# Sending the rows of two attentions' factors through DRAM instead of through TensorE, in a planned graph-and-slice transformer layer

## The chip, the core and the metric

The kernel runs on one core of a Trainium2 chip. The metric is device time in microseconds (us) from the start to the end of one execution; of several runs the median is taken. The profile is of one more execution.

## What is computed

The input x has 32 batch items of 512 nodes with 256 features, in fp32; adj is a 512 x 512 mask shared by all. One layer of a graph network and one of a slice transformer follow each other, each with a residual connection:

```python
def _gat(inp, adj_mask, W, a):
    h = inp @ W
    f1, f2 = h @ a[:F, 0], h @ a[F:, 0]
    e = leaky_relu(f1[:, :, None] + f2[:, None, :], 0.2)
    if adj_mask is not None:
        e = where(adj_mask[None] > 0, e, NEG_INF)
    return elu(softmax(e, axis=2) @ h)

def gnn(x):                       # 256 -> 512 -> 256 features
    out = residual = relu(x @ mlp1_w + mlp1_b)
    out = elu(_gat(relu(out), None, W_fc, a_fc)) + residual
    out = residual = relu(out @ mlp2_w + mlp2_b)
    out = elu(_gat(relu(out), adj, W_hand, a_hand)) + residual
    return relu(out)

def ffn(x):                       # 8 heads of 64, 64 slices
    w = softmax((x_mid @ W_slice + b_slice) / temp)     # 512 nodes x 64 slices, per head
    tokens = (fx_mid.T-weighted sums over the nodes) / (sums of w + 1e-5)
    out_slice = attention(tokens @ W_q, tokens @ W_k, tokens @ W_v)
    return (w @ out_slice, heads joined) @ W_out + b_out

x = x + gnn(layernorm(x), adj)
x = x + ffn(layernorm(x))
```

What matters for this change: both attentions add a number of the row's node (f1) and a number of the column's node (f2). A number that lies one to a node, so one to a partition, is at some point needed along a row of 512, the same in all 128 partitions. That is what is called spreading a factor here.

## The kernel before

**The work of one batch item.** `front(b)` loads x, does the first layernorm, mlp1, the product h with a Strassen scheme (seven products instead of eight), the factors, the attention matrix pT in a separable form and its product with h (pv, Strassen again). `middle(b, o1T)` does mlp2, the product h2, the masked attention e, its transposition p2T and the product pv2. `back(b, x1)` does the second layernorm, the slice weights w, the sums, the tokens, the small attention, and the output. Each part sets `nc.step`, one of 22 names from "load" to "out".

**Layout.** A tile has 128 partitions; the 512 nodes are NT = 4 to a partition: node 4p + t lies in partition p, place t, for x and the output. Transposes of large tiles are made without TensorE in the 30 batches other than the first and the last (`by_dma(what, b)` is true for them): VectorE transposes blocks of 32 x 32 (`flip`) into a stage, and `gather` writes the stage to DRAM by four DMAs and reads it back by one. For e this gives e_stage, scr and p2T. In the first and last batch TensorE transposes instead.

**How the factors are spread.** In the step "factors", f1 of the first attention is column HH of h, one number for each partition and place. VectorE adds f2's maximum to it (tile sc, 128 x 4), TensorE transposes each of the four columns, broadcast to 128, against the identity (tr<-ident,sc), and ScalarE reads the resulting PSUM tile pt, 128 x 512, into acb with two activations, then takes the exponential. In the step "h2" column D+1 of h2 goes the same way (tr<-ident,h) into a PSUM tile f2b; VectorE reads it directly for the four instructions that make e, each of which adds f2b to the mask mbias and keeps the row's maximum (e<-tr,mbias); only in the first and the last batch ScalarE first copies it to SBUF.

**What sets the order.** All operations are first recorded (`Recorder.take`; so the profile shows line 343 for nearly all of them), then `_schedule` puts them in one order with costs of its own: at each point it takes, of those that can start, the one with the lowest key, and no item may be more than three batches ahead of the oldest. A key is a due time: batch number times PERIOD, plus a value from the table TURNS by step and place in the step, plus shifts for the first and last three batches from HEAD and TAIL. SETUP holds the keys of the one-time preparations. Each engine then runs its instructions in that order and waits where an input or a buffer is not ready. So the table sets which work of four neighbouring batches stands beside which on every engine. In `emit`, within 120 us of the planned start or end, matmuls on the identity are put in where TensorE is planned to stand idle (`_fill`; line 351 in the profile).

**Queues.** Before the change all DMAs of the batches are issued by SP (SyncE); ScalarE issues two small ones at the very start.

Of the kernel before, what the change touches and what calls it, by code (L numbers as in the profile page):

```python
# [7 lines left out]
F32 = mybir.dt.float32  # L8
I32 = mybir.dt.int32
BF16 = mybir.dt.bfloat16  # L10
AF = mybir.ActivationFunctionType
OP = mybir.AluOpType
# [2 lines left out]
ENGINES = ("tensor", "vector", "scalar", "gpsimd", "sync")  # L15

TURNS = {
    "load": (-104.13,),
    "norm1": (5.81, -12.2, -0.38, 40.46, 5.49, 6.82, -28.3, -97.35, 73.26, 2141.3, -17.24, 7.8,
        -3.21, -61.78, -29.05, -31.03, -34.36, -3.93, -211.23, -208.37, -208.62, -207.57,  # L20
        -202.44),
    "mlp1": (44.88, -14.78, 475.5, -0.81, 29.84, 144.85, 30.48, 28.34, 46.7, 63.76, 30.7,
        163.15),
    "h": (217.43, 239.71, 301.88, 219.38, 228.31, 232.52, 223.78, 123.55, -183.63, -198.06,
        235.55, 281.78, 134.23, 84.93, 296.28, 284.15, 228.15, 213.81, 208.35, 40.76, -192.43,
        -208.97, 324.43, 90.08, 232.1, 162.36, 264.44, 305, 269.96, 302.11, 159.39, 131.88,
        217.06, 97.44, 286.09, 265.51, 197.21, 172.48, 330.83, 139.13, 316.66, 332.6, 199.8,
        210.03, 184.56, 233.17, 252.5, 357.26, 288.33, 243.5, 272.56, 242.46, 243.89, 262.61,
        301.12, 303.21),
    "factors": (1172.98, 68.61, 957.87, 880.81, 833.88, -94.89, 162.9, 564.16, 443.05, 632.16,  # L30
        99.22, 41.55, 117.2, -36.09, 151.35, 166.12, 162.03),
    "p": (-217.52, 222.09, -214.68, 156.3, -232.9, 226.84, -201.59, 222.19),
    "pv": (181.62, 173.02, 113.17, 168.75, 130.31, 121.86, 154.04, 91.05, 128.61, 93.43, 156.55,
        170.07, 249.5, 203.18, 183.65, 209.43, 161.93, 146.07, 129.44, 175.77, 84.33, 98.64,
        193.99, 67.43, 82.92, 77.34, 188.5, 225.33, 179.85, 196.17, 141.96, 66.83, 209.82,
        122.72, 185.96, 166.17, 256.1, 208.95, 191.25, 109.15, 168.68, 33.05, 111.29, 31.79,
        223.06, 225.68, 0.25, 146.41, 143.11, 131.52, 150.56, 135.14, 171.77, 185.87, 148.08,
        129.9, 112.28, 230.93, 210.68, 202.98, 108.67, 123.15, 135.98, 121.57, 427.87, 287.12,
        306.19, 126.95, 47.96, 44.6, 23.6, 354.94, 212.32, 233.37, 145.94, -25.73, 89.65, 87.01,
        301.3, 340.74),  # L40
    "o1": (175.72, 146.36, 318.31, 75.22, 202.48, -123.71, -11.06, -130.7, -287.11),
    "mlp2": (163.2, 216.89, 255.93, 271.92, 60.63, 285.36, 184.81, 130.74, 28.96, 65.99),
    "h2": (154.01, 126.18, 171.55, 124.34, 108.59, 78.41, 169.3, 89.79, 186.32, 157.35, 180.91,
        192.19, 105.96, 124.57, 26.13, 58.76),
    "e": (226.55, 172.24, 227.68, 199.08, 187.7, 234.17, 190.31, 206.45, 237.64, 232.92, 168.72,
        256.08, 408.52, 421.68, 391.27, 262.45, 442.54, 455.27, 273.82, 234.38, 519.53, 170.71,
        164.48, 31.36),
    "p2": (-14.68, 22.01, 55.59, 61.1, 56.92, -11.8, 67.6, 558.07, 85.28, 48.17, 40.53, 30.86,
        19.78, -12.55),
    "pv2": (231.3, 86.58, 94.48, 97.84, -101.11, 186.76, 109.51, 61.52, 85.01, -131.77, -150.14,  # L50
        205.52, 259.66, 267.31, 237.42, -131.44, -160, -120.69, -132.24, 154.68, 148.6, 111.83,
        139, -129.21, 152.77, 106.35, 144.25, 119.14, -162.13, -156.66, 273.74, 322.31, 325.93,
        361.68, -139.88, -151.25, -142.85, -161.55),
    "norm2": (3024.02, 107.62, 108.82, 88.2, 97.55, 53.73, 74.18, 49.61, 117.29, 3167.28,
        180.18, 68.34, 64.85, 86, 21.41, 8.51, 60.74, 13.84, 28.42, 83.96, 129.51, 212.73,
        234.97, 261.11, 2822.4, 116.47),
    "w": (305.34, 272.53, 290.14, 845.93, 798.64, 795.47, 283.65, 884.75, 926.27, 320.18, 751.4,
        375.01, 408.12, 405.42, 336.46, 305.77, 323.75, 367.7, 1201.11, 1138.46, 1563.38,
        745.63, 1124.55, 865.97, 1179.02, 980.75, 363.54, 428.69, 395.78, 437.6, 334.39, 367.5,
        367.07, 981.88, 934.2, 840, 174.53, 1035.96, 203, 1037.78, 1034.98, 480.9, 411.92,  # L60
        442.36, 358.87, 346.56, 246.11, 386.64, 1234.45, 758.39, 808.64, 610.85, 681.86, 882.99,
        492.47, 722.21, 414.99, 446.77, 335.28, 249.32),
    "sums": (219.1, 219.58, 227.77, 239.7, 383.95, 249.92, 251.57, 239.42, 242.03, 1077.37,
        1977.83, 234.3, 1454.25, 735.43, 2640.86, 592.26, 423.25, 660.64, -9.73),
    "s1T": (108.57, 368.64, 346.43, 140.99, 183.21, 126.3),
    "tokens": (328.88, 276.03, 298.43, 280.34, 354.01, 226.15, 295.4, 216.36, 344.5, 310.56,
        213.27, 259.2, 166.72, 280.67, 245.65, 277.29, 211.49, 312.02, 299.07, 271.19, 138.52,
        257, 235.11, 203.31, 251.8, 264.98, 212.57),
    "att": (205559.95, 208057.13, 394.33, 51833.74, 297.35, 190333.7, 260689.92, 418216.35),
    "vo": (374.47, 235.14, 638.61, 320.05, 321.87, 373.17, 345.11, 230.64, 163.72, 211.34,  # L70
        232.93, 232.76, 169.48, 276.17, 419.48, 556.46),
    "gg": (-50.95, -63.34, -63.34, -51.08, -78.74, -66.07, -40.3, -20.46, 150.92, 121.98),
    "out": (158.85, 78.08, -2.92, 6.88, -44.11, -73.16, -25.26, -4.67, 103.63, 87.34, -10.37,
        24.58, -12.49, 48.01, 59.4, 101.43, 136.08, 81.21, 268.69),
}
PERIOD, SPARE = 80.54, 0.01

HEAD = (
    (-61, -359, 0, 40, 0, 69, -1262, 189, -43, 457, -8, -24, 143, 947, 108, 718, -48, 6, 1, -39,
     119, -20),  # L80
    (168, 1, 0, 0, 0, 4, 174, 0, 144, -26, 75, 433, 58, 166, 0, 117, 154, 0, -183, -48, -372,
     1721),
    (172, 728, 1325, 0, -59, -269, -21, 34, -18, -363, 2035, 398, 404, -24, 1613, -199, 25,
     -134, 0, -3, -46, -85),
)
TAIL = (
    (36, 0, -352, 1, 67, 0, -772, 105, -24, 0, -312, 50, -6, -235, 1896, 375, 54, 83, -211, 13,
     -147, -271),
    (18, -170, -262, -383, 0, 42, 11, -11, -950, 795, -14, -10, -1671, -108, -157, 653, 6, 18,
     0, 210, 2, 652),  # L90
    (-4, -40, 0, -69, 10, -43, -630, -53, 276, -593, -1, -10, -589, 151, 299, 42, 316, 15, 89,
     4, -160, 43),
)


SETUP = (791.3598735632129, 2808.359873563213, 4385.359873563213, 9205.359873563213, 6407.359873563213, 3020.359873563213, 4840.359873563213, 5931.359873563213)

FLIPPED = ("xn", "u", "e", "o2", "w", "xn2")

P = 128  # L100
ALPHA = 0.2
MASKED = -(2.0 ** 55)
# [288 lines left out]
def adj_ffn_kernel(  # L391
# [26 lines left out]
    B, N, D = x.shape  # L418
    HID = mlp1_w.shape[1]
    HH = HID // 2  # L420
    NT = N // P
# [15 lines left out]
    def ts(i, n=P):  # L437
        return slice(i * n, (i + 1) * n)

    def new(name, shape, bufs=1, tag=None, dtype=F32):  # L440
        return sbuf.tile(list(shape), dtype, name=name, tag=tag or name, bufs=bufs)
# [4 lines left out]
    def tr_tile(shape):  # L446
        return psum.tile(shape, F32, tag="bank", name="tr", bufs=8)
# [11 lines left out]
    def by_dma(what, b):  # L459

        return what in FLIPPED and b not in EDGES
# [22 lines left out]
    def row(name, shape=(P, 512), tag=None):  # L484
        return new(name, shape, bufs=2, tag=tag)

    def small(name, shape):
        return new(name, shape, bufs=3)
# [249 lines left out]
            u if to is None else m, m, -1.0, u, op0=OP.add, op1=OP.max  # L738
        )

    def front(b):

        nc.step = "load"
# [72 lines left out]
        nc.vector.tensor_copy(f2[:, 2:], h22[:, :, HH])  # L816
        nc.step = "factors"

        fm = small("fm", [P, 1])
        nc.vector.tensor_reduce(fm, f2, axis=AX.X, op=OP.max)  # L820
        pf = sm_tile([P, P])
# [4 lines left out]


        beta = 1.0 - ALPHA
        sc = small("sc", [P, NT])
        nc.vector.tensor_scalar(sc, f1, f2m, None, op0=OP.add)  # L830
        ex = small("ex", [P, 2, NT])
        nc.vector.tensor_scalar(ex[:, 0], f2, f2m, None, op0=OP.subtract)
        nc.vector.tensor_scalar(ex[:, 1], f2, f2m, ALPHA, op0=OP.subtract, op1=OP.mult)
# [3 lines left out]
        nc.vector.memset(h1[:, :, HH], -1.0)  # L837
        nc.vector.memset(h2[:, :, HH], 1.0)

        pt = tr_tile([P, N])  # L840
        for i in range(NT):
            nc.tensor.transpose(pt[:, ts(i)], sc[:, i : i + 1].to_broadcast([P, P]), ident)
        acb = new("acb", [P, 2, N], tag="xnT")
        nc.scalar.activation(acb[:, 0, :], pt, AF.Relu, scale=-beta)
        nc.scalar.activation(acb[:, 1, :], pt, AF.Relu, scale=beta)
        nc.scalar.activation(acb, acb, AF.Exp, scale=-1.0)

        nc.step = "p"
# [61 lines left out]
    def middle(b, o1T):  # L910
# [17 lines left out]
                    pm, o2T[:, k, ts(t)], wh[:, k, :], start=(k == 0), stop=(k == KD - 1)  # L928
                )
            nc.scalar.copy(h[:, t, :], pm)  # L930
        f2b = tr_tile([P, N])
        for j in range(NT):
            nc.tensor.transpose(f2b[:, ts(j)], h[:, j, D + 1 : D + 2].to_broadcast([P, P]), ident)
        if not by_dma("e", b):
            pt, f2b = f2b, new("f2b", [P, N], tag="acb")
            nc.scalar.copy(f2b, pt)
        nc.step = "e"
        pT = new("p2T", [P, NT, N], tag="pT" if b == B - 1 else None)
        if by_dma("e", b):
# [2 lines left out]
        masked = [new("e", [P, N + 2], bufs=4)[:, :N] for i in range(NT)]  # L942
        for i, e in enumerate(masked):
            nc.vector.tensor_tensor_reduce(
                out=e, in0=f2b, in1=mbias[:, i, :], scale=1.0, scalar=3.0 * MASKED,
                op0=OP.add, op1=OP.max, accum_out=top[:, i : i + 1],
            )
        nc.vector.tensor_tensor(top, top, f1, op=OP.add)
# [341 lines left out]
```

## Time and profile before

| | us |
|---|---|
| median of 3 runs | 2467.51 (2467.47 to 2471.15) |
| the profiled execution's own time | 2464.71 |
| its span, first to last instruction | 2462.9 |

| engine | busy, us | share |
|---|---|---|
| PE (TensorE matmuls) | 2442.5 | 99% |
| PEld (weight loads, beside PE) | 1705.3 | 69% |
| DVE (VectorE) | 2096.1 | 85% |
| ACT (ScalarE) | 1428.9 | 58% |
| POOL (GpSimd) | 116.8 | 5% |

A group of instructions is named by what it writes and reads, out<-in, with numbers left out: mm<-wh,o2T is the product h2, mm<-h,p2T is pv2, mm<-h,pT and the like pv, mm<-gg,wT the output, mm<-weff,xn2T w, mm<-w,xn the sums. A matmul in fp32 takes two passes and counts as two instructions; a transpose takes one. Durations of neighbouring matmuls overlap, so times on PE are read from the distance of starts. SPq marks DMA issues of SP. In the chain of waits each piece gives its start, its length and what the engine did.

### The profile page before, as it was taken

What the parts mean: (1) busy time and instruction counts of PE and PEld (TensorE: products, weight loads), DVE (VectorE), ACT (ScalarE), POOL (GpSimd) and SP (SyncE); (2) the same over time, 40 slices, a digit from 0 to 9 for tenths busy, and PEclk for the clock granted to TensorE, in tenths of its full rate; (3) what the DMA queues carried; (4) which work ended last, traced back from release to release, by engine and by line L of the source; (5) the groups of instructions that cost most, each with busy time, mean ns of one, the idle gap of its engine ahead of it and who ended that gap; (6) DMA issues with size and microseconds to landing.
All of it is one profiled execution on the core that took longest, in us unless ns stands there. A gap on an engine that the chain in (4) does not pass through costs nothing.

```text
span 2462.9 us, 35296 instructions
## 1 busy us (share of the span) xinstructions
PE 2442.5 (99%) x11607; PEld 1705.3 (69%) x11607; DVE 2096.1 (85%) x5636; ACT 1428.9 (58%) x3319; POOL 116.8 (5%) x184
## 2 busy tenths in 40 slices
PE   9999999999999999999999999999999999999999
PEld 7766667666676767676766676766767676767666
DVE  8688798888898888898888888888988888998775
ACT  2665556656556555566565566565565555665564
POOL 4000000000000000000000000000000000000000
PEclk9999999999999999999999999999999999999999
DMA  5133565455565455655555664556654556645531
GB/s 176 35 93 100 154 165 163 126 160 140 157 165 144 133 147 149 163 165 136 149 144 144 165 164 130 156 139 154 168 146 134 147 150 161 163 127 143 139 106 54
DMA packets 450047, 348.11 MB, mean 141 GB/s; under 512 B 109381, under 2 KB 374469, under 8 KB 449864
## 3 DMA queue, kind: packets, MB, share of 16 engines
q1 hardware_dynamic: 449334, 345.85, 51.8%
q8 instruction: 92, 1.51, 0.2%
q14 instruction: 91, 0.75, 0.1%
q10 hardware_dynamic: 530, 0.01, 0.0%
HBM read 186.27 MB, written 159.45 MB: 140 GB/s over the span
## 4 chain that ended last, share of the span: by engine, by line
PE 86%; DVE 3%; DMA 2%; ACT 0%; issue 0%; SPq 0%; DVEq 0%
PE mm L343 83%; PE tr L343 3%; DMA p2T<-scr 1%; DVE e L343 0%; DMA rn<-line 0%; DVE v L343 0%; DMA o1T<-scr 0%; SPq L343 0%; DVE e_stage L343 0%; DVE gg L343 0%; DMA scr<-e_stage 0%; DVE mx L343 0%; DVE pT L343 0%; DVE rs L343 0%; DVE xn_stage L343 0%
## 5 line engine op out<-in xcount | busy, mean ns | idle before, releaser
L343 ACT ACTIVATE w<-mm,mx 128x64 f32<-128x64 f32 x1024 | 231.1, 346 | 41.7 <-DVE mx L343 41.7
L343 PE MATMUL mm<-weff,xn2T 128*128 128x512 f32 x512 | 247.2, 598 | 0.5 <-ACT xn2T L343 0.5
L343 PE MATMUL mm<-w,xn 128*128 128x512 f32 x512 | 235.9, 593 | 3.5 <-DVE w L343 3.5
L343 PE MATMUL mm<-o1T,w 128*128 128x512 f32 x512 | 235.1, 593 | 1.3 <-DVE o1T L343 1.3
L343 PE MATMUL mm<-h,p2T 128*128 128x257 f32 x1024 | 232.5, 380 | 0.9 <-DMA p2T<-scr 0.9
L343 PE MATMUL mm<-gg,wT 128*128 128x256 f32 x1024 | 231.4, 382 | 0.2 <-DVE gg L343 0.2
L343 PE MATMUL mm<-xnT,w 128*128 128x512 f32 x512 | 225.9, 593 | 0.5 <-ACT xnT L343 0.4
L343 PEld LDWEIGHTS mm<-h,p2T 128*128 128x128 f32 x1024 | 193.7, 189 | 42.5 <-issue 14.5
L343 PEld LDWEIGHTS mm<-gg,wT 128*128 128x128 f32 x1024 | 190.0, 190 | 46.4 <-DVE gg L343 22.1
L343 ACT ACTIVATE v<-v,rd 128x512 f32<-128x512 f32 x128 | 90.5, 713 | 172.9 <-DVE rd L343 172.9
L343 PEld LDWEIGHTS mm<-xnT,w 128*128 128x128 f32 x512 | 96.9, 190 | 119.2 <-issue 111.2
L343 ACT ACTIVATE above<-e,top 128x512 f32<-128x512 f32 x128 | 88.4, 720 | 126.1 <-DVE top L343 109.4
L343 PEld LDWEIGHTS mm<-w,xn 128*128 128x128 f32 x512 | 96.1, 190 | 87.9 <-issue 72.3
L343 PEld LDWEIGHTS mm<-o1T,w 128*128 128x128 f32 x512 | 94.6, 190 | 85.9 <-issue 73.4
L343 PEld LDWEIGHTS mm<-weff,xn2T 128*128 128x128 f32 x512 | 93.8, 189 | 70.4 <-issue 56.4
L343 PEld LDWEIGHTS mm<-h,pT 128*128 128x128 f32 x512 | 96.3, 189 | 64.6 <-issue 37.9
L343 ACT ACTIVATE m<-m,neg 128x512 f32<-128x512 f32 x192 | 137.3, 717 | 1.3
L343 PE MATMUL mm<-h,pT 128*128 128x257 f32 x512 | 134.6, 380 | 3.4 <-DVE pT L343 3.4
L343 DVE TENSOR_TENSOR v<-mm,v 128x256 f32<-128x256 f32 (+1 forms) x320 | 127.7, 409 | 3.5 <-PE mm L343 1.7
L343 PE MATMUL mm<-wh,o2T 128*128 128x258 f32 x512 | 127.4, 382 | 0.0
L343 PE MATMUL mm<-h,pmix 128*128 128x256 f32 x512 | 125.8, 378 | 0.0
L343 PE MATMUL mm<-wfc,o0T 128*128 128x257 f32 x512 | 125.0, 385 | 0.0
(191 smaller groups left out, 5002.2 us busy)
## 6 DMA issues: line engine op xcount, KB each, us to landing
scr<-xn_stage SPq DMA_DIRECT2D x240, 128.0 KB, 3.0
scr<-u_stage SPq DMA_DIRECT2D x120, 256.0 KB, 4.4
o1T<-scr SPq DMA_DIRECT2D x30, 1024.0 KB, 7.6
scr<-e_stage SPq DMA_DIRECT2D x120, 256.0 KB, 4.3
p2T<-scr SPq DMA_DIRECT2D x30, 1024.0 KB, 5.4
scr<-w_stage SPq DMA_DIRECT2D x120, 256.0 KB, 4.0
w_raw<-scr SPq DMA_DIRECT2D x30, 1024.0 KB, 7.8
x<-in_x_dram SPq DMA_DIRECT2D x32, 512.0 KB, 4.2
```

Of the source, the lines that this page charges most:

```text
L343: getattr(getattr(self.nc, op.engine), op.method)(*op.args, **op.kwargs)
```

## The change

In the 30 middle batches both factors are spread by two DMAs from ScalarE's queue instead of by four transposes: `spread` writes the 128 x 4 column tile to a line of 512 numbers in DRAM (16 bytes from each partition), and reads that line into each of 128 partitions (2 KB each, tiles f1_row and f2_row, one buffer each). Since the line holds node 4p + t at its place in order, it is read with a step of four elements: `(i t) -> t i`. In the first and the last batch the transposes stay.

For the first attention sc is now f1 alone, copied before f2's maximum is known, and the maximum enters as a bias (fb, two columns) of ScalarE's two activations. For the second a small tile g2 is copied out of h2 first. The four instructions of e read f2_row from SBUF.

All of TURNS, PERIOD, HEAD, TAIL and SETUP is new. The shifts in HEAD and TAIL are nearly all zero, and PERIOD goes from 80.54 to 75.21.

```diff
-PERIOD, SPARE = 80.54, 0.01
+PERIOD, SPARE = 75.21301149425301, 0.01
...
+    def spread(name, col):
+
+        line = dram.tile([P, NT], F32, name="line", tag=name + "_line", bufs=2)
+        nc.scalar.dma_start(line, col)
+        wide = new(name + "_row", [P, N])
+        nc.scalar.dma_start(
+            wide, bass.AP(tensor=line.tensor, offset=line.offset, ap=[[0, P], [1, N]])
+        )
+        return wide.rearrange("p (i t) -> p t i", t=NT)
...
         nc.step = "factors"
 
+        sc = small("sc", [P, NT])
+        nc.vector.tensor_copy(sc, f1)
+        if by_dma("u", b):
+            pt = spread("f1", sc)
         fm = small("fm", [P, 1])
...
-        sc = small("sc", [P, NT])
-        nc.vector.tensor_scalar(sc, f1, f2m, None, op0=OP.add)
+        fb = small("fb", [P, 2])
+        for s, slope in enumerate((-beta, beta)):
+            nc.vector.tensor_scalar(fb[:, s : s + 1], f2m, slope, None, op0=OP.mult)
...
-        pt = tr_tile([P, N])
-        for i in range(NT):
-            nc.tensor.transpose(pt[:, ts(i)], sc[:, i : i + 1].to_broadcast([P, P]), ident)
+        if not by_dma("u", b):
+            pt = tr_tile([P, N])
+            for i in range(NT):
+                nc.tensor.transpose(pt[:, ts(i)], sc[:, i : i + 1].to_broadcast([P, P]), ident)
+            pt = pt.rearrange("p (t i) -> p t i", t=NT)
         acb = new("acb", [P, 2, N], tag="xnT")
-        nc.scalar.activation(acb[:, 0, :], pt, AF.Relu, scale=-beta)
-        nc.scalar.activation(acb[:, 1, :], pt, AF.Relu, scale=beta)
+        for s, slope in enumerate((-beta, beta)):
+            nc.scalar.activation(
+                acb[:, s, :].rearrange("p (t i) -> p t i", t=NT), pt, AF.Relu,
+                bias=fb[:, s : s + 1], scale=slope,
+            )
...
-        f2b = tr_tile([P, N])
-        for j in range(NT):
-            nc.tensor.transpose(f2b[:, ts(j)], h[:, j, D + 1 : D + 2].to_broadcast([P, P]), ident)
-        if not by_dma("e", b):
-            pt, f2b = f2b, new("f2b", [P, N], tag="acb")
+        if by_dma("e", b):
+            f2 = small("g2", [P, NT])
+            nc.vector.tensor_copy(f2, h[:, :, D + 1])
+            f2b = spread("f2", f2)
+        else:
+            pt, f2b = tr_tile([P, N]), row("f2b", tag="u")
+            for j in range(NT):
+                nc.tensor.transpose(
+                    pt[:, ts(j)], h[:, j, D + 1 : D + 2].to_broadcast([P, P]), ident
+                )
             nc.scalar.copy(f2b, pt)
+            f2b = f2b.rearrange("p (t i) -> p t i", t=NT)
...
             nc.vector.tensor_tensor_reduce(
-                out=e, in0=f2b, in1=mbias[:, i, :], scale=1.0, scalar=3.0 * MASKED,
+                out=e.rearrange("p (t i) -> p t i", t=NT), in0=f2b,
+                in1=mbias[:, i, :].rearrange("p (t i) -> p t i", t=NT), scale=1.0, scalar=3.0 * MASKED,
                 op0=OP.add, op1=OP.max, accum_out=top[:, i : i + 1],
             )
```

## The prediction

> **What bounds the kernel now.** First the page's engine line and the table of stretches. PE is busy in all of a middle period, DVE in 65.3 of its 74.6 us, ACT in 44.2.
>
> ```profile
> PE 2442.5 (99%) x11607; PEld 1705.3 (69%) x11607; DVE 2096.1 (85%) x5636; ACT 1428.9 (58%) x3319; POOL 116.8 (5%) x184
> ```
>
> ```profile
> core 0: us, PE busy (x) PEld busy (x) DVE busy (x) ACT busy (x) POOL busy (x), PEclk, DMA share, GB/s
> ...
> 1196.10:1270.70 74.60, 74.60 (x353) 51.83 (x353) 65.29 (x176) 44.18 (x104) 2.91 (x5) 1.00 0.56 150
> ```
>
> Second the chain that ended last: the same piece of matmuls comes back every 74.68 us, one batch, and nearly all of it is PE.
>
> ```profile
> 1121.38 63.52 PE mm L343 x278
> 1196.07 63.52 PE mm L343 x278
> 1270.75 63.52 PE mm L343 x278
> ```
>
> 23 such periods lie between 374.58 and 2092.99; 32 times 74.68 are 2389.8 of the span of 2462.9. So a saved PE pass counts at once, until another loop is as long as the period. The candidate is the second attention: from the last pass of h2 (mm<-wh,o2T) over e, the exchange through DRAM and back to the first mm<-h,p2T. The timelines of PE, DVE and SP give its points:
>
> ```profile
> 1195.02 0.47 PE L343 MATMUL mm<-attT,tokT 64*64 64x64 f32 x16
> ...
> 1226.61 5.37 PE L343 MATMUL mm<-h,p2T 128*128 128x257 f32 x24
> ```
>
> ```profile
> 1196.11 0.69 DVE L343 CUSTOM_DVE_ANT_0 e<-tr,mbias 128x512 f32<-128x512 f32 x1 [0.26 <-PE tr L343]
> ...
> 1212.73 0.69 DVE L343 STREAM_TRANSPOSE e_stage<-e 128x512 f32<-128x512 f32 x1
> ```
>
> ```profile
> 1213.45 3.38 SPq L343 DMA_DIRECT2D scr<-e_stage  x4
> 1220.44 0.38 SPq L343 DMA_DIRECT2D p2T<-scr  x1
> ```
>
> h2 ends at 1195.02, e runs from 1196.11 to 1213.42, and p2T, issued at 1220.44 and landing after 5.4 us (its median), is there at 1225.84, **0.8 us before PE asks for it** at 1226.61. In one period the chain of waits shows this loop running out:
>
> ```profile
> 1364.76 4.92 DMA scr<-e_stage
> 1369.70 6.76 DMA p2T<-scr
> 1376.46 0.14 issue
> 1376.59 8.47 PE mm L343 x35
> ```
>
> 1226.61 plus two periods is 1375.97, so PE began 0.6 us late there.
>
> [...] SP stood 124.6 us in 29 waits for line<-norm, the same construction. [...] The trace of before has no such read on DVE or ACT; on POOL the one read at that step (mbias<-adjt) takes 2.11 us beside 0.83 for mbias<-mbias, in other types.
>
> **The change part by part.** (a) In 30 batches four transposes of sc and four of h2's last column go. Pieces of four transposes take 0.44 us in the chain of waits, so 8 x 0.11 = 0.87 us a batch, 26 us in all, on PE: the floor of the period becomes 73.81.
>
> (b) ACT loses nothing (in the 30 middle batches DVE read f2b from PSUM without a copy) and gains four DMA issues a batch. The two ACT issues at the start of the trace took 0.47 and 0.49 us; line<-norm, with the same pieces of 16 bytes, 1.06 on SP at the median. So 2 to 3 us of ACT's 30 idle ones. Behind the waiting f1_row issue stand xn2's two copies and o2T's relu, which PE needs for h2; behind line<-g2 stand two pT, a few exps and the copy of mean, which PE needs for mm<-wvo,mean. By the order of instructions these have about 0.3 us to spare, so I put 0 to 0.6 us a period, and take 0.2.
>
> (c) The pair of DMAs. norm<-s1T, equally 2 KB, lands after 2.8 us; the broadcast m<-W_fx, equally 128x512 from one row, after 3.3, in the quiet start. f1's loop (h to pT's matmuls) has mlp2, h2, w, wvo, out and half of sums on PE between, 29 us at the steps of (d), and needs about 11 (issue 0.5, the DMAs 6.1, acb 2.2, pT 1.3, signals); those hide it. f2's isn't roomy. Its loop in the new order of instructions: fourth h2 copy behind attT's 0.8; g2 0.3; line issue 0.5; two pT, mean and eight exps on ACT (3.2) end at 4.8, later than the line's landing (1.1 + 2.8 = 3.9); f2_row's landing 3.3 and the signal give 8.3. DVE from the first e to the last flip, at the steps of its timeline: four e 2.4, four max 2.3, five flips 3.1, three statistics 1.0, two mx 1.2, two w 1.2, two x1 1.2, rs and pmix 1.2, small ones 0.5: 14.1, to 22.4 (before, 17.3, with pT and gg between). From the last flip to p2T's landing as before, 1213.42 to 1225.84: 12.4. **Sum 34.8.**
>
> (d) What PE does meanwhile in the new order, counted at the steps of the PE timeline: 32 passes of 512 (w, sums) at 0.43, 13.8; 32 of out, 7.05; 56 of the Strassen product of pv at 0.217, 12.15; wvo 1.04, attT 0.40, tokens 1.08, a transpose 0.11: **35.6**. So p2T would be 0.8 us early, if nothing of (c) is slower than its nearest row.
>
> (e) Reads with a step of 16 bytes: four e (0.61 us a step) and two acb (0.55). Between nothing and a doubling: 0 to 2.4 us on the e loop, and 0 to 1.1 on acb, of which ACT's idle time before h2's copies hides most (0 to 0.3 remain). [...] I take half, 1.2 and 0.1: nothing shown favours an end. The 256 KB of f2_row meets r<-scr and the o2 writes: 0 to 1 us, I take 0.5.
>
> Late by 1.2 + 0.1 + 0.5 - 0.8 = 1.0; with 0.2 from (b) the period is 73.81 + 1.2 = 75.0, 0.3 over before, in 30 batches **+10 us**.
>
> (f) The new table. Middle periods are again alike, so the head and tail remain. The instruction stream holds 72 warm-up matmuls at the start (71 before), but 73 near the end where there were 23, 26 of them half wide: a row of seven took 1.76 us (L351, 0.25 each), so 24 x 0.25 + 26 x 0.13 = **9 us** more, standing where PE has nothing else. From 0 (they fill waits that before had without filling) to 20.
>
> (g) The rest: two fb and g2 on DVE, 0.2 us each, in DVE's 9 idle us; 15 MB more DMA beside 348; no SP DMA is added. Nothing, unless DVE becomes the late one.
>
> Sum: 2462.9 + 10 + 9 = 2482 span; the profiled execution's own time is 1.8 above its span, and the median of the runs another 2.8 above that: **2487**.
>
> **The rivals.** *Floor reached.* The 16-byte step costs nothing and both DMAs land as in (c): only (b) remains, 74.0. 30 x -0.67 = -20, +9: 2452 span, 2456. For it: PE holds every middle period, and the loop has 0.8 us. Against: two unmeasured costs, both upward. It decides where f2's loop stays under 35.6 us. *Doubled reads.* e takes 1.2 us: late by 2.4 + 0.3 + 0.5 - 0.8 = 2.4, period 76.4, +52 +9: 2524 span, 2528. [...] *Balance.* Half the penalty without the contention: period 74.5, -5 +9: 2467 span, 2471. *ACT's queue*: (b) at its upper end on top of the forecast, 0.4 us a period more: 2499, inside the forecast's range. That the rows don't go by DMA can't be: the new order of instructions has two such pairs for each of the 30 batches.
>
> **How the numbers follow.** Forecast 0.36 with a range of its own from 2474 to 2503 (with the ACT case); floor 0.29, faster by more than 0.2% (5 us, about what a measurement can tell from no change); balance 0.12, mostly within; doubled 0.23. Faster 0.29, same 0.11, slower 0.60. Best of the floor case with no tail loss, 2447; doubled, 2528.
>
> **What would show it.** Period of the repeated piece 75.0; PE's idle before mm<-h,p2T put down to DMA p2T<-scr, about 1 us a period (now 0.9 in all for PE); e's mean 0.9 to 1.0 us from 0.684, acb's above 0.6; f2_row landing at 3.3 to 4.3; more L351 time at the end. The forecast is wrong if e keeps 0.68 and the period is at 74 or below, or if the wait stands before wvo,mean instead.

## The result: 2577.6 us, 4.4% slower

The changed kernel takes 2577.6 us (median of 4 runs, 2572.14 to 2578.2) where the kernel before, beside it, takes 2468.22: a ratio of 1.0436 [1.0418, 1.0454]. The profiled execution took 2577.58 us with a span of 2575.5, so the span grew by 112.6. The prediction (2487; its forecast from 2474 to 2503, its rivals from 2447 to 2528) had the direction and far too small a size.

The first lines to read are again the engine line and the shares of the chain that ended last.

```profile
PE 2491.2 (97%) x11479; PEld 1698.5 (66%) x11479; DVE 2152.4 (84%) x5730; ACT 1442.0 (56%) x3319; POOL 125.1 (5%) x184
```

```profile
PE 48%; DVE 21%; ACT 14%; DMA 14%; issue 3%; SPq 1%; POOL 0%; ACTq 0%; DVEq 0%; POOLq 0%
```

PE executes 128 instructions fewer (240 transposes are gone, 112 passes of filling on the identity are added; in the trace of before an fp32 matmul stands as two instructions, mm<-weff,xn2T x512 for 256 calls, and a transpose as one, tr<-ident,h x128 for 128) and yet shows 48.7 us more of busy time. Its share of the chain, 86% before, is 48%: DVE, ACT and DMA now hold half of the path. To see where the time lies, the span is cut at the first matmul of mm<-h,p2T of each of the 32 batches, read from the PE timelines.

| kernel | start to first | 31 distances | last to end | mean distance, 22 middle batches |
|---|---|---|---|---|
| before | 111.4 | 2291.1 | 60.4 | 74.72 |
| after | 124.3 | 2378.3 | 72.9 | 77.46 |

25 us lie at the two ends and 87 in the middle; a period of 75.0 was forecast. In the middle, the timeline of PE in one period of after shows where it stands still (start, length, and in brackets the idle time and what ended it):

```profile
1090.10 1.88 PE L334 MATMUL mm<-weff,xn2T 128*128 128x512 f32 x4
1092.31 0.48 PE L334 MATMUL mm<-attT,tokT 64*64 64x64 f32 x16 [0.33 <-ACT attT L334]
...
1093.78 1.59 PE L334 MATMUL mm<-wvo,mean 64*64 64x256 f32 x16
1095.30 1.12 PE L334 MATMUL mm<-weff,xn2T 128*128 128x512 f32 x2
...
1103.17 3.60 PE L334 MATMUL mm<-weff,xn2T 128*128 128x512 f32 x8
1107.94 3.67 PE L334 MATMUL mm<-w,xn 128*128 128x512 f32 x8 [1.18 <-DVE top L334]
...
1128.72 7.12 PE L334 MATMUL mm<-h,p2T 128*128 128x257 f32 x32
```

PE waits for attT (ACT) and before the sums mm<-w,xn (put down to DVE's top, which stands behind the four e). Before mm<-h,p2T, where the prediction put the wait, there is none. The list of PE's waits over the whole run (us in total, times, longest) says the same:

```profile
PE mm L334 <- DVE top L334: 27.6, 28, 1.8
PE mm L334 <- ACT attT L334: 9.3, 29, 0.5
PE mm L334 <- ACT w L334: 8.2, 29, 2.6
...
PE mm L334 <- DMA p2T<-scr: 2.1, 5, 1.5
```

The groups by form give count, busy us and mean ns of the two reads of the spread rows, first before, then after:

```profile
L343 DVE CUSTOM_DVE_ANT_0 e<-tr,mbias 128x512 f32<-128x512 f32 x120 | 80.2, 684 | 6.8 <-PE tr L343 6.8
L343 ACT ACTIVATE acb<-tr 128x512 f32<-128x512 f32 x64 | 34.7, 594 | 3.2 <-PE tr L343 1.5
```

```profile
L334 DVE CUSTOM_DVE_ANT_0 e<-f_row,mbias 128x512 f32<-128x512 f32 x120 | 128.5, 1072 | 6.0 <-DMA f_row<-line 5.6
L334 ACT ACTIVATE acb<-f_row,fb 128x512 f32<-128x512 f32 x60 | 72.7, 1218 | 0.6 <-DMA f_row<-line 0.5
```

e takes 1072 ns a piece (before 684) and acb 1218 (before 594), both of which read PSUM before and SBUF now. The list of DMA issues gives KB each and the median time to landing, near the nearest rows that the prediction used:

```profile
f_row<-line ACTq DMA_DIRECT2D x60, 256.0 KB, 3.3
...
line<-sc ACTq DMA_DIRECT2D x30, 2.0 KB, 2.1
line<-g ACTq DMA_DIRECT2D x30, 2.0 KB, 3.4
```

### The profile page after: what moved, and what is told of

Read it like the earlier page. It is cut to its first block, busy times and chain, and to the rows that moved or that the text cites. A ratio compares the mean times of both kernels' runs of the same rounds, so it can differ in the third digit from the quotient of the medians.

```text
span 2575.5 us, 35443 instructions
## 1 busy us (share of the span) xinstructions
PE 2491.2 (97%) x11479; PEld 1698.5 (66%) x11479; DVE 2152.4 (84%) x5730; ACT 1442.0 (56%) x3319; POOL 125.1 (5%) x184
## 4 chain that ended last, share of the span: by engine, by line
PE 48%; DVE 21%; ACT 14%; DMA 14%; issue 3%; SPq 1%; POOL 0%; ACTq 0%; DVEq 0%; POOLq 0%
PE mm L334 46%; DVE e L334 6%; ACT acb L334 4%; ACT w L334 2%; DMA scr<-xn_stage 2%; DMA f_row<-line 2%; DMA scr<-e_stage 2%; ACT above L334 2%; DVE pmix L334 2%; DMA xnT<-scr 2%; DMA line<-g 2%; PE tr L334 2%; ACT e L334 2%; DVE x L334 1%; DVE rs L334 1%
## 5 line engine op out<-in xcount | busy, mean ns | idle before, releaser
L334 ACT ACTIVATE w<-mm,mx 128x64 f32<-128x64 f32 x1024 | 239.6, 341 | 74.6 <-DVE mx L334 74.2
L334 PE MATMUL mm<-w,xn 128*128 128x512 f32 x512 | 233.9, 596 | 27.9 <-DVE top L334 27.6
L334 PE MATMUL mm<-o1T,w 128*128 128x512 f32 x512 | 241.3, 599 | 0.4 <-DVE o1T L334 0.4
L334 DVE SCALAR_TENSOR_TENSOR pT<-acb,ex,pT 128x512 f32<-128x512 f32 x128 | 93.7, 754 | 115.2 <-ACT pT L334 114.8
L334 ACT ACTIVATE sc<-sc 128x256 f32<-128x256 f32 x32 | 13.3, 417 | 246.6 <-DVE sc L334 246.6
L334 PE MATMUL mm<-hx,pmix 128*128 128x256 f32 (+1 forms) x512 | 129.5, 397 | 12.5 <-ACT w L334 8.2
L334 PE MATMUL mm<-mixed,mix 128*128 128x257 f32 x512 | 135.1, 388 | 0.0
L334 DVE CUSTOM_DVE_ANT_0 e<-f_row,mbias 128x512 f32<-128x512 f32 x120 | 128.5, 1072 | 6.0 <-DMA f_row<-line 5.6
L334 PE MATMUL mm<-wfc,mix 128*128 128x257 f32 x512 | 132.3, 379 | 0.0
```

The lines of the kernel that those rows point to most:

```text
L334: getattr(getattr(self.nc, op.engine), op.method)(*op.args, **op.kwargs)
```

## The experiments

Three suspects were separated: the reads with a step of 16 bytes, the pair of DMAs, and the new order of the work with its table. Theory A at the start: nearly all of the excess over the forecast is the step. In e1, e2, e3, e6, e7, e9 and e10 some elements of the rows belong to other nodes, so these kernels don't compute the layer; e4, e5, e8, e11 and e12 do. The mean distance is that of one profiled execution. Times below are medians; each ratio is to the kernel before in the same series.

| kernel | us | ratio [95%] | mean distance |
|---|---|---|---|
| e1: no step | 2506.73 | 1.0161 [1.0146, 1.0176] | 75.05 |
| e2: no step for e | 2525.26 | 1.0237 [1.0222, 1.0253] | 75.77 |
| e3: no step for acb | 2552.15 | 1.0344 [1.0329, 1.0359] | 76.69 |
| e4: the table alone | 2529.43 | 1.0252 [1.0235, 1.0269] | 75.92 |
| e5: pieces of 4 bytes, no step | 2921.2 | 1.1841 [1.1823, 1.1858] | 89.21 |
| e6: a step of 8 bytes | 2505.54 | 1.0154 [1.0139, 1.0169] | 75.01 |
| e7: rows don't wait for the line | 2567.54 | 1.0410 [1.0395, 1.0426] | 77.06 |
| e8: e5 with the old table | 3530.06 | 1.4297 [1.4251, 1.4343] | |
| e9: e1, one due time moved | 2526.7 | 1.0245 [1.0231, 1.0259] | 75.88 |
| e10: e1 and e7 together | 2502.19 | 1.0149 [1.0135, 1.0163] | 75.11 |
| e11: the change with the old table | 3186.27 | 1.2918 [1.2900, 1.2935] | 97.26 |
| e12: no filling at the end | 2585.24 | 1.0484 [1.0470, 1.0499] | 77.32 |

**e1, e2, e3: the step taken away**, for both rows, for f2 alone (e), for f1 alone (acb). The row is then read as it lies. The traces of the three have PE's, ACT's and DVE's instructions in after's order, apart from at most two neighbours on DVE.

```diff
-        return wide.rearrange("p (i t) -> p t i", t=NT)
+        return wide.rearrange("p (t i) -> p t i", t=NT)
```

> Both rows are read contiguously instead of with a step of 16 bytes, in the same order of instructions on every engine (the elements then belong to other nodes; only the order of elements within a row is changed). Theory A, the step carries the loss of the middle periods: acb back from 1.217 to about 0.67 us, e from 1.07 to 0.68; both lie in series in the loop from h2 to the PSUM banks that the w exponentials free, 2 x 0.55 + 4 x 0.39 = 2.65 us a period, so the period goes from 77.3 to 74.7 and the time from 2577 to about 2503. Theory B, the DMA pair and the order of the new table carry it: the period stays above 76.5, 2555 or more. Theory C, the head and tail of the table carry it: the period was not the trouble, 2560.

> Only f2's row is read contiguously (the order of elements within that row is changed); f1's keeps its step. Theory A: 4 x 0.39 = 1.56 us a period less, period 75.7, about 2533. Theory B: 2565 to 2577.

> Only f1's row is read contiguously (the order of elements within that row is changed); f2's keeps its step. Theory A with acb in series: 2 x 0.55 = 1.1 us a period less, period 76.2, about 2547. If ACT's idle time hid acb, as the prediction had it (0 to 0.3 left): 2570 to 2577.

Without the step 70.9 us of the 109 are gone. The groups of e1, the same two lines as of after:

```profile
L334 DVE CUSTOM_DVE_ANT_0 e<-f_row,mbias 128x512 f32<-128x512 f32 x120 | 81.8, 682 | 1.0 <-DMA f_row<-line 0.9
...
L334 ACT ACTIVATE acb<-f_row,fb 128x512 f32<-128x512 f32 x60 | 42.4, 711 | 0.1
```

So the step costs 0.39 us on each of four e and 0.51 on each of two acb: 1.56 + 1.01 = 2.57 us of work a batch. The period fell by 77.46 - 75.05 = 2.41: **nearly none of this is hidden**. The single runs add up to it: over e1, e's step alone adds 1.64 to the period (e3), acb's alone 0.72 (e2). So e's 1.56 us come through whole, and of acb's 1.01 about 0.3 are hidden. The timeline of PE in e1, at the same stretch, shows the idle time gone:

```profile
1061.82 1.88 PE L334 MATMUL mm<-weff,xn2T 128*128 128x512 f32 x4
1063.63 0.47 PE L334 MATMUL mm<-attT,tokT 64*64 64x64 f32 x16
1064.04 1.12 PE L334 MATMUL mm<-weff,xn2T 128*128 128x512 f32 x2
1065.09 1.11 PE L334 MATMUL mm<-wvo,mean 64*64 64x256 f32 x16
1066.13 1.13 PE L334 MATMUL mm<-weff,xn2T 128*128 128x512 f32 x2
...
1074.15 3.60 PE L334 MATMUL mm<-weff,xn2T 128*128 128x512 f32 x8
1077.58 3.60 PE L334 MATMUL mm<-w,xn 128*128 128x512 f32 x8
```

From start to start: weff to attT 1.81 us (the piece itself is shown 1.88 long, so neighbours overlap) where after has 2.21; wvo 1.04, not 1.52; the eight weff to w,xn 3.43, not 4.77. These three differences are 2.2 of the 2.41. No idle time is shown inside wvo, but in after ACT's copy of mean, which wvo reads, runs from 1093.97 to 1094.22, while the wvo passes have begun at 1093.78. Why acb is hardly hidden is read on the timeline of ACT in after (the work between the lines is left out):

```profile
1086.60 0.69 ACT L334 ACTIVATE o2T<-mm,b 128x512 f32<-128x512 f32 x1 [1.26 <-PE mm L334]
1087.19 1.23 ACT L334 ACTIVATE acb<-f_row,fb 128x512 f32<-128x512 f32 x1
...
1091.85 0.41 ACT L334 COPY attT<-tr 128x256 f32<-128x256 f32 x1
```

and at the same place in e1:

```profile
1132.85 0.69 ACT L334 ACTIVATE o2T<-mm,b 128x512 f32<-128x512 f32 x1 [1.26 <-PE mm L334]
1133.43 0.71 ACT L334 ACTIVATE acb<-f_row,fb 128x512 f32<-128x512 f32 x1
...
1137.10 0.39 ACT L334 COPY attT<-tr 128x256 f32<-128x256 f32 x1
```

ACT has 1.26 us of idle time in both, but it lies ahead of o2T's relu, which waits for PE; the two acb stand behind that, back to back with h2's copies and attT. In these two periods attT starts 5.25 us after the relu in after and 4.25 in e1: here the whole 1.0 us.

**e4: the table alone**, with both rows made by TensorE's transposes.

```diff
-        if by_dma("u", b):
+        if False:
             pt = spread("f1", sc)
...
-        if not by_dma("u", b):
+        if True:
             pt = tr_tile([P, N])
...
-        if by_dma("e", b):
+        if False:
             f2 = small("g2", [P, NT])
...
-            nc.scalar.copy(f2b, pt)
+            f2b = pt
+            if not by_dma("e", b):
+                f2b = row("f2b", tag="u")
+                nc.scalar.copy(f2b, pt)
```

> The new table, with both rows spread by TensorE's transposes as before (no DMA from ACT). Theory A: the table itself is sound in the middle, period near 74.7, and only head and tail cost, about 29 us: 2495. Theory B (the new order of instructions is worse in the middle whatever the spread): period above 76, 2540 or more. If the table costs nothing at all: 2468.

Theory A's number fell here, though Theory B's 2540 and period above 76 were not quite reached: with the old spreading, the order that the new table makes costs 62 us. It keeps PE on the chain that ended last:

```profile
PE 92%; DVE 4%; ACT 2%; DMA 2%; issue 0%; SPq 0%; POOL 0%; DVEq 0%; ACTq 0%
```

The periods of 75.92 us are 1.2 longer than before, and the two ends together 25.0 us longer. Against e4 the kernel with spreading by DMA and unstepped reads (e1) is 22.7 us faster; its period is shorter by 0.87. So the result can be written as a sum of three: from 2468, +62 for the table, -23 for the spreading, +71 for the step. Only the last is a clean difference. With transposes to place, the scheduler makes another order from the same table: in e4 many instructions of PE, DVE and ACT stand elsewhere than in e1, so the -23 holds a change of order too.

e4 also splits acb's growth. It reads PSUM as before did, but in the changed form with the bias, and takes 683 ns; of the way from 594 to 1218, 89 ns come with that form, 28 with the row in SBUF (e1, 711), and 507 with the step.

**e5: a complete kernel without the step.** The line is written in the order in which it is read, in 512 pieces of 4 bytes.

```diff
-        line = dram.tile([P, NT], F32, name="line", tag=name + "_line", bufs=2)
-        nc.scalar.dma_start(line, col)
+        line = dram.tile([NT, P], F32, name="line", tag=name + "_line", bufs=2)
+        nc.scalar.dma_start(line.rearrange("t p -> p t"), col)
...
-        return wide.rearrange("p (i t) -> p t i", t=NT)
+        return wide.rearrange("p (t i) -> p t i", t=NT)
```

> A complete version of the contiguous read: the line in DRAM is kept place by place, so it is written in 512 pieces of 4 bytes instead of 128 of 16 bytes, and the row is read without a step; the order of instructions is that of the changed kernel. If the writing in smaller pieces costs nothing on the path: the time of e1_unit_both, 2507. If 512 pieces take 1 us longer to land, f2's loop is that much longer in each of 30 batches: 2530. Above 2577 the pieces would be worse than the step.

The third case came true, and far beyond its 2577: 2921 us. The list of DMA issues of e5 has the cause:

```profile
line<-sc ACTq DMA_DIRECT2D x30, 2.0 KB, 8.3
line<-g ACTq DMA_DIRECT2D x30, 2.0 KB, 8.6
```

The same 2 KB land after 8.3 and 8.6 us in place of 2.1 and 3.4. How this reaches PE is in the waits of e5. ACT holds each row's DMA until its line has landed, and the work behind it in ACT's order waits too:

```profile
ACT xn2T L334 <- DMA line<-sc: 175.5, 28, 8.0
ACT w L334 <- DMA line<-g: 128.2, 23, 6.7
```

In after the first was 2.3 us in 2 waits and the second isn't in the list. PE in e5 waits 136.3 us for o2T, which stands behind xn2T on ACT, and 132.6 for top; in e itself DVE waited 149.6 us for f_row, in after 5.6. Five to six us more for each of two lines would make 11.4 of the 14.2 us by which the period stands above e1's, if both count in full; the rest is open, and the granted clock was lower too (0.937, in e1 0.997). So the loops have some room for the pair of DMAs, and not 6 us more for each line.

**e6: a step of 8 bytes**, each read then taking every second element of most of the row, some of them twice.

```diff
-        return wide.rearrange("p (i t) -> p t i", t=NT)
+        return bass.AP(
+            tensor=wide.tensor, offset=wide.offset, ap=[wide.ap[0], [N // 8, NT], [2, P]]
+        )
```

> Both rows are read with a step of two elements (8 bytes) instead of four (the elements then belong to other nodes, some twice), in the same order of instructions. [...] acb 0.71 and e 0.68 us, time 2507 as with no step. [...] acb about 0.96, e about 0.88, time near 2540. If any step is slow: as the changed kernel, 2577.

2505.54 us, the interval overlapping e1's. The groups:

```profile
L334 DVE CUSTOM_DVE_ANT_0 e<-f_row,mbias 128x512 f32<-128x512 f32 x120 | 81.4, 679 | 0.9 <-DMA f_row<-line 0.9
...
L334 ACT ACTIVATE acb<-f_row,fb 128x512 f32<-128x512 f32 x60 | 45.2, 760 | 0.0
```

e is as short as without a step (679 ns, in e1 682); acb takes 0.05 us more (760 ns, in e1 711). So a step as such need not be slow: with 16 bytes these two took 1072 and 1218 ns (after), with 8 they didn't come near that. Other steps were not tried.

**e7 and e10: the pair of DMAs taken out of the loop.** The line is still written; the rows are filled from mlp1_b instead, so they wait for nothing of the batch. e7 keeps the step, e10 reads the row as it lies.

```diff
+        other = bass.AP(tensor=mlp1_b.tensor, offset=mlp1_b.offset, ap=[[0, P], [1, N]])
+        nc.ops[-1].args = (wide, other)
         return wide.rearrange("p (i t) -> p t i", t=NT)
```

> The line is still written, but both rows are read from an input of 512 numbers instead of from the line, so their DMA need not wait for the line's landing (the factors of the rows are then other numbers); the step of 16 bytes and the order of instructions stay. If the pair of dependent DMAs is in f2's loop: about 3 us of landing fall out of it, the period falls to where acb alone leaves it, 75.5 to 76.5: 2520 to 2550. If only the reads with a step matter and the row is there in time anyway: 2570 to 2577.

> The changed kernel with both rows read without a step and from an input (mlp1_b) instead of the line just written, which is still written: so neither the step nor the pair of DMAs is in any loop; values in the rows are not the factors. Order as in the changed kernel. Theory A (without the step, the 0.5 us a period left over the wait-free 74.53 are waits of the second attention's loop, in which the pair of DMAs stands): the period falls to 74.5, 16 us under e1's 2506.7: 2491. Rival B (what is left is the order's own, the DMAs are hidden): 2504 to 2509.

e7 is 10 us under after, with intervals that just overlap; e10 is at e1's time within the intervals, and its period (75.11) is no shorter, though that was read from the slowest of its four executions (2508.05). Its median lies 2 us under Rival B's range and 11 over Theory A: with the step away, the pair costs nothing that these runs can tell. What makes up the 0.5 us a period by which e1 stands above its wait-free 74.53 stays open. In e7, PE still waits before the sums, 21.3 us of after's 27.6:

```profile
PE mm L334 <- DVE top L334: 21.3, 28, 1.3
```

The chain of after has both ways of closing. In one period the pair of DMAs is on it:

```profile
1092.77 4.31 DMA line<-g
...
1097.10 3.12 DMA f_row<-line
...
1100.24 1.07 DVE e L334
```

and in the period before it is not; the chain goes from acb over attT, PE and gg into e on DVE (the DVE work between gg and e is left out):

```profile
1010.28 1.23 ACT acb L334
...
1015.08 0.28 ACT attT L334
...
1015.40 2.63 PE mm L334 x28
...
1018.06 1.29 DVE gg L334 x2
...
1023.01 0.99 DVE e L334
```

Two paths meet at DVE's e, and e7 suggests that they are nearly of one length: with the pair removed, the other holds. Both carry the stepped acb and e, which fits with the removal of the step paying in full.

**e9: one due time of the new table**, on top of e1.

```diff
-        211.08, 211.11, 211.18, 211.21, 211.24, 216.79),
+        211.08, 211.11, 211.18, 211.21, 211.24, 211.27),
```

> The changed kernel with the rows read without a step (as in e1, 2506.7 us), and one number of the new table moved: the eighth quarter of tr<-tok,q gets the due time of its neighbours, 211.27 in place of 216.79, so that TensorE does the 64 x 64 transposes of a batch in one group instead of in two. Theory A (part of what the new order costs by itself is small matmuls put singly among full ones): the single pair takes 0.25 us to the next start where it takes 0.05 in its group, and the pair of full matmuls before it 0.96 instead of 0.86, so 0.30 us a period go, 31 times: 9 us, 2497.5 us. Rival B (the place where matmuls stand costs nothing, the 0.3 us are made of something else): 2506.7 within 2 us. Rival C (the move delays something behind it): above 2509.

The small effect is there: on the PE timelines the 16 passes of tr<-tok,q take 0.39 us to the next start in one group, where e1 has 0.40 for 14 and another 0.25 for the last 2. But the kernel is 20 us slower (Rival C), as the waits of PE in e9 show:

```profile
PE mm L334 <- ACT v L334: 20.8, 30, 1.6
```

In e1 the wait for v came 3 times, 3.1 us in all. A single moved due time gave the scheduler another order of DVE's and PE's work well beyond the moved pair, and with it a new wait in nearly each batch that is larger than the gain. So e9 doesn't say what the grouping alone is worth.

**e8 and e11: the old table kept.** e11 is the change with TURNS, PERIOD, HEAD, TAIL and SETUP of before; e8 is that with the lines of e5 and unstepped reads.

> The table, PERIOD, HEAD, TAIL and SETUP of the kernel before, with both rows spread by DMA and read without a step. If the old table would have carried the spread: 26 us of PE saved, 2445 to 2460. If its due times, made for transposes, put the consumers too early: PE waits for the two rows, several us a period: 2550 to 2700.

> The change without its table: the spreading by DMA with pieces of 16 bytes and the stepped reads as in the changed kernel, but TURNS, PERIOD, HEAD, TAIL and SETUP as before. Theory A (in the old order both loops are tight: e had 0.8 us to spare, and the pair of DMAs adds 2.8 + 3.3 us, twice a batch, plus 2.6 us of the step): some 15 us a period, 30 times: 2800 to 2950. Rival B (only the second attention's loop is tight): 6.1 + 1.6 - 0.8 = 7 us a period, 2680. Rival C (the scheduler's own costs let it move enough work in between): under 2600, or even under the changed kernel's 2577.

Both missed upwards, e8 (3530 us) by 830 us and e11 (3186) by more than 200. In e11's chain the pair of DMAs stands on the path, with what follows it:

```profile
1222.46 0.18 DVE g L343
1222.67 2.31 DMA line<-g
1224.98 1.23 ACT w L343 x6
...
1226.52 4.30 DMA f_row<-line
...
1230.84 0.04 DVE e L343
```

The row's issue stands in ACT's order behind exponentials of w, and comes 1.5 us after the line has landed; e begins 8.4 us after g. The first attention waits too: PE's longest wait in e11 is for pT, 207.2 us in 27 times, where before had 3.4. The period is 97.26 us. Why it grew 7 us more than both loops of Theory A together is not settled; the granted clock was also lower there (0.908). The comparison says that the new table is what makes the two DMAs cheap: 3186 against 2577.6 us.

**e12: no filling near the end.**

```diff
-                if fresh and gap > 0.7 and not self.FILL < op.start < last - self.FILL:
+                if fresh and gap > 0.7 and op.start <= self.FILL:
```

> The changed kernel without the warm-up matmuls near the end (73 matmuls on the identity, 6 to 9 us of TensorE's time by their distance of starts); those at the start stay. Theory A (they stand in waits that are there anyway; the longer end is the order's own): 2575 to 2580, no change. Rival B (they delay the work behind them, as the prediction took it): 2568 to 2572. Rival C (without them the granted clock falls at the end): above 2580.

2585.24 us: a ratio of 1.0484 [1.0470, 1.0499] against after's 1.0436 [1.0418, 1.0454], so slower by some 0.5%, as Rival C had it. The loss lies in the end. These are the stretches from the last batch's first mm<-h,p2T to the end, of after and of e12 (length, busy time of PE, PEld, DVE, ACT and POOL, granted clock, DMA share, GB/s):

```profile
2502.60:2575.50 72.90, 64.85 (x446) 46.93 (x446) 30.65 (x79) 23.19 (x66) 1.37 (x3) 0.99 0.16 46
```

```profile
2500.80:2581.50 80.70, 61.20 (x344) 39.84 (x344) 30.64 (x79) 23.41 (x66) 1.37 (x3) 0.83 0.15 41
```

Without the filling the stretch is 7.8 us longer, at a granted clock of 0.83 in place of 0.99, while the 31 distances are the same within 1 us. The filling is not what makes the end longer than before; it helps.

No version beat the kernel before. e10, e6 and e1 come nearest, 35 to 39 us behind it, and none of the three computes the layer; the complete kernels without the step, e5 and e8, are far behind. What was left without the step is the table's cost less what the spreading saves.

## Why the prediction was wrong

**The PE saving (a) was right in kind.** The eight transposes a batch are gone and were put at 0.87 us. From e4 to e1 the mean period falls by just that, 0.87, and the time by 22.7 us, against 26; but the order of the work changes between the two as well, so a match as close as this may be partly luck.

**The ACT queue (b) and the DMAs (c) were about right.** ACT's four issues take 0.33 us each, 1.3 us a batch, under the 2 to 3 taken, and ACT's work behind a row's issue waited 2.3 us for a line's landing in the whole run, where 0.2 a period was taken. f_row lands after 3.3 us as taken, line<-g after 3.4 where 2.8 was taken. The 0.5 us put down for f2_row's meeting with other transfers was the author's estimate, and was not shown. That the room in these loops is small was right in kind: e5's 5 to 6 us more per line went through, and in e7 and e10 the pair was worth some 10 us at most.

**Step (e), the stepped reads, is the term that failed most, and twice.** First the size: it took 1.2 us a batch for e and 0.1 for acb, with bounds at 2.4 and 0.3, and let 0.8 us of spare time at p2T absorb a part. Measured in the period are 1.64 for e (e3) and 0.72 for acb (e2), 2.41 together (e1), 71 us in all. The e term lay inside its bounds and was a quarter too small. The acb term lay outside: the prediction compared 1.1 us with ACT's *idle time before h2's copies* and let it hide. That idle time stands before o2T's relu, ahead of acb, and can't be used by what comes after it. Second the place: the loop was followed from e to p2T alone. PE does not wait there, so the 0.8 us absorbed nothing. It waits where ACT and DVE, busy with the longer reads, hand over attT, mean, top and w. Part of this is the sign that the prediction itself named as speaking against it, a wait at mm<-wvo,mean; its other sign, e at 0.68 us with a period of 74 or below, did not come.

Nothing in the trace of before showed what a step of 16 bytes costs on DVE or ACT, and its one row at this step, POOL's mbias<-adjt, is of other types: the range from nothing to a doubling was the author's estimate. The runs give the size for these two instructions. With the step (after) e takes 1072 ns where it takes 682 without (e1), 57% longer, and acb 1218 where it takes 711, 71% longer. Half the step doesn't cost half of that: in e6 e takes 679 ns and acb 760.

**Step (d), what PE does in a period, took the old durations into the new order.** It put the floor at 73.81, and one period of e1 in which PE shows no wait, 1061.82 to 1136.35, is 74.53. If the 0.87 are saved, the order itself costs 0.72. The timelines of e1 and e9 show one part of that: a pair of 64 x 64 transposes put alone among full matmuls takes 0.25 us to the next start instead of 0.05. The pairs of weff between attT, wvo and gg (1.05 and 0.96 us from start to start, where two such passes elsewhere take 0.86, in e1 3.43 for eight) are another, argued from the timelines and not tried.

**Step (f), the ends, was mis-sized and wrongly explained.** 9 us were taken for added filling. The ends of e1, e4 and after are 25.0 to 25.4 us longer than before's, and e12 shows that the filling is no loss. What makes the head 12.8 and the tail 12.5 us longer in after was not tried; HEAD and TAIL, which shifted the first and last batches before, are nearly zero now. A part of the head may be the clock: the granted clock in the first 124.3 us of after is 0.96, in the first 111.4 us of before 1.00, which by estimate from these figures is worth 5 us at most.

**In the sum**, the forecast had +19 us of span, of which +10 in the middle periods. Measured: +25 at the ends, then in the 31 distances +40 for the order (e4), -24 from e4 to e1 (39.9 to 16.4 us over before), +71 for the step (16.4 to 87.2). The rival *doubled reads*, 2528 us, was nearest in mechanism. Its 2.7 us a period for the step are more than the 2.41 measured, since too much for e made up for too little for acb. It was still 50 us short: like the forecast it took off 0.8 us of spare time, counted from the floor of 73.81 and gave the table nothing but 9 us at the ends.

## What to carry to other kernels

Price a new access pattern on every instruction that reads through it, and before calling it hidden, check on the timeline that the idle time stands *behind* the slowed instruction and ahead of what waits for its engine. When a change brings a new order of work, the order is a change of its own: run it alone with the old code, since here it cost 62 us where the step cost 71, and was also what made the DMAs cheap. Where two paths of nearly one length meet, taking one away shows little (10 us in e7); look for what both carry. A DMA that must wait for another holds up whatever stands behind it in the order of the engine that issues it: in e5 xn2T on ACT waited 175.5 us in 28 times for line<-sc, up to 8.0 at once.

## What was not expected of the hardware

- A read of 512 fp32 numbers from SBUF with a step of 16 bytes takes 1.07 us on DVE (e) and 1.22 on ACT (acb) in after, against 0.68 and 0.71 without a step in e1; with a step of 8 bytes it takes 0.68 and 0.76 (e6).
- The same activation from PSUM takes 0.68 us with a bias column (e4) and 0.59 without (before); the way the 512 elements are addressed differs too, and the two were not tried apart.
- Writing 2 KB from 128 partitions to DRAM lands at the median after 2.1 us (line<-sc) and 3.4 (line<-g) in pieces of 16 bytes (after), and after 8.3 and 8.6 in pieces of 4 (e5).
- Where 64 x 64 passes stand among full matmuls (e1), PE's starts are 0.1 to 0.2 us further apart at each place, with no wait shown in the trace: 0.25 us for a pair of tr<-tok,q alone, where its group of 16 in e9 takes 0.39, or 0.05 a pair; 1.05 and 0.96 for two passes of weff beside attT, wvo and gg, where two elsewhere take 0.86. The cause was not tried.
